# A Swin block and a dynamic convolution on one core: the first three rounds written out as one list, with cheaper weight folds and the early keys on ScalarE

## The chip, the cores and the metric

The kernel runs on one core of a Trainium2 chip. The metric is the device time of one execution in microseconds (us), from the first to the last instruction with what lies around them. The core has five engines with a queue each: TensorE (PE; its weight loads are PEld), VectorE (DVE), ScalarE (ACT), GpSimd (POOL) and SyncE (SP), which here only issues DMAs. All arithmetic is in float32.

## What is computed

The input is a batch of 16 images of 192 channels and 56 x 56 pixels. First comes a shifted-window attention block with its MLP, then a depthwise 3 x 3 convolution whose weights are computed from the image itself. Cut to what matters:

```python
# layer 0: shifted windows of 7 x 7, 6 heads of 32 channels
h = roll(layernorm(x over channels), -3, -3)          # norm 1
q, k, v = windows(h) @ qkv_w + qkv_b
a = softmax(q @ k.T * SCALE + rel_bias + window_mask)
x1 = x + roll(windows_back((a @ v) @ proj_w + proj_b), 3, 3)
y = gelu(layernorm(x1) @ fc1_w + fc1_b)               # norm 2
x2 = x1 + y @ fc2_w + fc2_b
# layer 1: masked depthwise 3 x 3 with weights per image and channel
t = relu(batchnorm(mean(x2 over pixels) @ w1.T))
taps = (t @ w2.T + b2) * mask                         # 4 of 9 taps stay
out = depthwise_conv(x2, taps) + bias
```

## The kernel before

**Tiling.** An image is cut into four steps; a step is two bands of seven rows (one row of windows each), so there are 64 steps. A tile has 128 partitions: one band on the first 64 (row half 0), the other on the last 64 (row half 1), and the 192 channels as three groups `g` of 64. Most products therefore use a half of TensorE's rows (`tile_position=(64 * ab, 0)`), and the two halves are issued in turn.

**Stages of a step s.** Norm 1: `statistics(0, s)` (L303) squares the rows on ScalarE and folds the three groups on GpSimd. Then the norm's product: either `full_deviations` (L392), which leaves mean and mean square on all 128 partitions (L398), after which ScalarE and VectorE make the reciprocal deviation in `rb` there; or `deviations(norms)` (L323), which does one or two norms in a few lanes (L333) and spreads them by a round trip through DRAM (one store, two loads on SP). `scaled1` (L435) multiplies the rows by it on GpSimd (L447, and L458 for the window that wraps round). `queries_keys` (L481) has three parts (products at L489): 0, queries of heads 0 to 3, copied by ScalarE (L502); 1, their keys, copied twice and masked by VectorE (L513); 2, heads 4 and 5, copied by ScalarE (L526, L536) and VectorE (L545). `scores` (L555) has three blocks j: product (L571), bias and maximum on VectorE (L597, L608), subtraction on GpSimd (L613), exponential on ScalarE (L620), sum and reciprocal on VectorE (L625, L626), share on GpSimd (L631). `turn_shares` (L635) turns them on VectorE (L642) and moves them by ten DMAs to `pt` (L648). `values` (L666) makes v in three groups (L686, copied by ScalarE, L702) and moves it by eight DMAs (L712); `turn_values` turns it (L721). `weighted` (L724) multiplies shares and values (L741), copied out by ScalarE (L768) or VectorE (L770). `biased_rows` (L779) adds a bias to the rows; `projection` (L786) multiplies (L812, L798) and VectorE adds to the rows (L840). Norm 2 is as norm 1, with `statistics(1, s)` and `scaled2` (L474). `first_layer` (L851, GELU at L863) and `second_layer` (L889) are the MLP; the convolution follows for each image.

**Weights.** The norms' gains and shifts are folded into the weights once. `centred_weights` (L1367) takes column means with products (L1378) and centres the weights on VectorE (L1407); `shift_steps` (L1338) multiplies weights by the norm's shift (products with one column, L1345), with the first row half only. `fold_qkv` and `fold_qkv_rest` do this for attention, `fold_v` (L1480) for the values' bias, `fold_fc1` for the first layer, and `fold_taps` prepares the convolution's weights.

**What sets the order.** The stages call `add(engine, planned duration, function, keys read, keys written)`. `Plan.order` then places all instructions: TensorE's stay in the order of the calls, the other engines take, at each moment of a planned timeline, a ready instruction by its latest due time. The order of the calls is therefore TensorE's order, and the planned durations and lags only steer the other queues. PSUM has four double banks, handed out in turn by `bank()`: a product waits until the one four banks earlier has been read. The calls come from a loop over rounds r from -2 (L1675): round r has scores and values of step r, the weighted sum and projection of step r - 1, the first layer of step r - 2 and the second layer of step r - 3. Rounds 0 to 2 deviate by many conditions (L1704 to L1780): the first steps use `full_deviations`, and step 0's third part of queries and keys stands between its second and third scores. `warm` (L193) issues products without use ahead of the first real ones.

Of the kernel before, what the change touches and what calls it, by code (L numbers as in the profile page):

```python
# [140 lines left out]
def tile_swin_then_dynamic_conv(  # L141
# [116 lines left out]
    mask2 = sb("mask2", 128, 2)  # L258
    km = sb("km", 128, 2)
    f1b = sb("f1b", 128, NFC)  # L260
    b1f = sb("b1f", 128, NFC)
# [219 lines left out]
    def queries_keys(s, parts):  # L481
        d = xs_of(s)[0]
        for i in parts:
# [26 lines left out]
            elif i == 1:  # L510
                for h in range(2):
                    def go(p=p, h=h):
                        nc.vector.tensor_scalar(  # L513
                            kbd[:, :, :, h, :],
                            p[:, :, 0:UT].rearrange("p a (w t) -> p a w t", t=N),
                            bq[:, 1:2],
                            mask2[:, h : h + 1],
                            ALU.add,
                            ALU.mult,
                        )  # L520
                    add("DVE", 1.0, go, [pk, "qb", "mask2"], [("kbd", h)])
# [32 lines left out]

    def scores(s, amid=None):  # L555

        last = s % NU == NU - 1
        for j in range(3):
            if j == 2 and amid is not None:
                amid()  # L560
            p, pk = bank()
# [70 lines left out]

            add("POOL", 1.9, share, [("tot", j)], [("e", j)])

    def turn_shares(s):  # L635
# [88 lines left out]
    def weighted(s):  # L724
# [25 lines left out]
        for j in range(3):  # L750
# [8 lines left out]
            for i in range(4):  # L759
# [5 lines left out]
                else:  # L765
                    dst = o2[lanes]
                if j != 1 or s < 2:
                    add("ACT", 0.5, lambda dst=dst, src=src: nc.scalar.copy(dst, src), [k], [("o", j, i)])  # L768
                else:
                    add("DVE", 0.56, lambda dst=dst, src=src: nc.vector.tensor_copy(dst, src), [k], [("o", j, i)])  # L770
# [566 lines left out]

    def shift_steps(n, chunks, p):  # L1338


        for c, lhs in enumerate(chunks):
            for g in range(G):
                to = 0
                for a in lhs(g):
                    nc.tensor.matmul(  # L1345
                        p[to : to + a.shape[1], 0, c : c + 1],
                        a,
                        vecs[0:64, 2 * n + 1, g : g + 1],
                        start=(g == 0),
                        stop=(g == G - 1),  # L1350
                        tile_position=(0, to),
                    )
                    to += a.shape[1]
            yield

    def shift_products(n, chunks, keys):
        p, pk = bank()
        add(
            "PE",
            0.68 * len(chunks),  # L1360
            lambda: list(shift_steps(n, chunks, p)),
            keys + [("vec", 2 * n + 1, 0)],
            [pk],
        )
        return p, pk

    def centred_weights(n, w, raw, keys, parts, chunks=()):  # L1367
# [3 lines left out]
        pm, mk = bank()  # L1371
        p, pk = bank() if chunks else (None, None)

        def means():
            shifts = shift_steps(n, chunks, p)
            for i, lo, hi, _ in parts:
                for g in range(G):
                    nc.tensor.matmul(  # L1378
# [6 lines left out]
                    )  # L1385
                    next(shifts, None)

        add(
            "PE",
            2.5 + 0.4 * len(chunks),  # L1390
            means,
            keys + [("gs", n)] + [("vec", 2 * n + 1, 0)] * bool(chunks),
            [mk, pk] if chunks else [mk],
        )

        for i, lo, hi, pieces_ in parts:
            for to, n_, view, done in pieces_:
                for g in range(G):
# [17 lines left out]
                    )  # L1416
        return p, pk

    qkv_keys = [("wqkvl", j) for j in range(2)]

    def fold_qkv():
# [24 lines left out]
        p, pk = shift_products(  # L1446
            0, [lambda g, i=i: [wraw[0:64, g, i * DIM : i * DIM + 128]] for i in range(2)], qkv_keys
        )

        def biases():  # L1450
            nc.vector.tensor_tensor(bq[:, 0:2], p[:, 0, 0:2], qkvb[:, 0:2], ALU.add)
            nc.vector.tensor_scalar(qbs[:, 0:1], bq[:, 0:1], SCALE, None, ALU.mult)

        add("DVE", 0.4, biases, [pk, "qkvb"], ["qb"])

    def fold_qkv_rest():
        p, pk = shift_products(
            0,
            [lambda g: [wraw[0:64, g, i * DIM + 128 : i * DIM + DIM] for i in range(2)]],
            qkv_keys,  # L1460
# [38 lines left out]
    def fold_fc1():  # L1499
        keys = [("wf1l", g, j) for g in range(G) for j in range(2)]  # L1500
        chunks = [lambda g, f=f: [wf1[0:64, g, f * 128 : (f + 1) * 128]] for f in range(NFC)]
        h = 2 * DIM
# [10 lines left out]
            0.2,  # L1513
            lambda: nc.vector.tensor_tensor(b1f, p[:, 0, 0:NFC], f1b, ALU.add),
            [pk, "f1b"],
# [150 lines left out]

    def last_heads():
        fold_qkv_rest()
        queries_keys(0, (2,))
        fold_v()  # L1670

    def has(s):
        return 0 <= s < S

    for r in range(-2, S + 3):  # L1675
        if r == -2:
            parameters_first()
            load(0, -100.0, 4.5)
            small_loads()
# [18 lines left out]
        if r == 0:  # L1698
            load(3)
            load_fc2()  # L1700
            load_taps()
        if has(r + 2) and r > -2:
            statistics(0, r + 2)
        early = r < 3  # L1704
        norms = [n for n, s in ((0, r + 2), (1, r - 1)) if has(s) and not early]
        if has(r) and r != 2:
            ahead = values(r)
            scores(r, {0: last_heads, 1: lambda: next(ahead)}.get(r))
            for _ in ahead:
                pass  # L1710
        if r == 2:
            scores(r)
            scaled1(3)
            queries_keys(3, (0, 1, 2))
            fold_fc1()
            full_deviations(1)
            scaled2(0)
            weighted(1)
        if r == 3:
            deviations([1])  # L1720
        if has(r - 2) and r > 2:
            scaled2(r - 2)
        if has(r + 1) and r > -2 and r != 2:
            if r == -1:
                warm(2, rb[:, 0], RB(0))
            scaled1(r + 1)
        if -2 < r < 2:
            if r == -1:
                warm(2, xs1[:, 0], [("xs1", 0)])
                queries_keys(0, (0, 1))  # L1730
            else:
                queries_keys(r + 1, (0, 1, 2))
            full_deviations()
        if has(r - 1) and r != 2:
            weighted(r - 1)
        if r == 1:
            ahead = values(2)
            for _ in range(G):
                next(ahead)
            fold_taps()  # L1740
        if has(r):
            turn_shares(r)
            turn_values()
        if r == 1:
            for _ in ahead:
                pass
        if r == S + 2:
# [15 lines left out]
        if has(r - 1):  # L1763
# [4 lines left out]
            statistics(1, r - 1)  # L1768
        if r == 2:
            full_deviations()  # L1770
        if weighing:
            halos(b)
        if not early and has(r + 1):
            queries_keys(r + 1, (0, 1, 2))
        if has(r - 2):
            table("gelu_and_others")
            first_layer(r - 2)
            table("natural_log_exp_and_others")
        if norms:
# [97 lines left out]
```

## Time and profile before

| | us |
|---|---|
| median of 3 runs (lowest, highest) | 2739.83 (2738.79, 2743.73) |
| the profiled execution | 2740.57 |
| its span, first to last instruction | 2738.5 |
| mean granted TensorE clock | 0.995 of full speed |
| VectorE, ScalarE, GpSimd busy | 1959.8, 1717.2, 1555.3 |
| first product of step 0's queries starts | 21.60 |
| first scores | 28.41 |
| first weighted sum | 67.35 |
| fold of the first layer's weights starts | 90.92 |
| first layer of step 0 starts | 114.38 |
| weighted sum of step 2 starts | 132.39 |

The rows with a start are from the trace, in us from the start of the span. A line of a view names a source line, the engine and what it writes and reads. A releaser ("<-") is what ended the idle time before an instruction. A matmul in float32 is recorded as two instructions, so 36 records of L489 are 18 products. Times come from one execution; the runs beside it lie within 5 us of each other.

### The profile page before, as it was taken

To read this page: it belongs to the slowest core of one execution; us is meant where nothing else is said; L and a number is where in the kernel's file an instruction comes from. 1 tells how busy PE (TensorE), PEld (TensorE's weight loads), DVE (VectorE), ACT (ScalarE), POOL (GpSimd) and SP (SyncE) were. 2 spreads that over 40 slices of the span, in tenths; PEclk is the share of its full clock that TensorE was granted. 3 is DMA by queue.
4 is the path that set the end of the run, shared out by engine and by line. 5 is a ranking of instruction groups with operands and counts; after the bars stand their busy time and mean duration, and the time that the engine had idled before them with its cause. 6 is when DMAs were issued, how large, how long until landed. Compare 5 with 4: busy or idle time off the path is not lost.

```text
span 2738.5 us, 78187 instructions
## 1 busy us (share of the span) xinstructions
PE 2707.5 (99%) x32911; PEld 1667.4 (61%) x32911; DVE 1959.8 (72%) x3457; ACT 1717.2 (63%) x2795; POOL 1555.3 (57%) x1433
## 2 busy tenths in 40 slices
PE   8999999999999999999999999999999999999998
PEld 5656656656666666566566566566566566666654
DVE  7656877767687676776767777676876767767674
ACT  4655666657666666666657666566666666676553
POOL 6656555555565565564565565565655655655532
PEclk9899999999999999999999999999999999999999
DMA  6522342434425334343344424344253343433231
GB/s 136 120 55 62 89 107 68 95 74 104 93 67 126 68 79 110 67 115 77 78 97 92 105 67 103 70 100 93 67 131 67 75 110 82 110 74 73 60 78 52
DMA packets 140603, 239.40 MB, mean 87 GB/s; under 512 B 34216, under 2 KB 98268, under 8 KB 140252
## 3 DMA queue, kind: packets, MB, share of 16 engines
q1 hardware_dynamic: 139100, 232.67, 37.9%
q8 instruction: 258, 4.23, 0.7%
q10 hardware_dynamic: 1152, 1.74, 0.3%
q14 instruction: 93, 0.76, 0.1%
HBM read 66.61 MB, written 38.98 MB: 39 GB/s over the span
## 4 chain that ended last, share of the span: by engine, by line
PE 96%; DVE 2%; DMA 1%; ACT 1%; SPq 0%; issue 0%; POOL 0%; ACTq 0%; DVEq 0%
PE ps L889 28%; PE ps L851 28%; PE ps L489 14%; PE ps L686 7%; PE ps L571 5%; PE ps L741 5%; PE ps L812 5%; PE ps L798 2%; PE ps L333 2%; DVE sq L985 0%; DMA x<-in_x_dram 0%; DVE x L840 0%; DVE hid L1165 0%; DVE trow L984 0%; ACT o L768 0%
## 5 line engine op out<-in xcount | busy, mean ns | idle before, releaser
L889 PE MATMUL ps<-hid,wf 128*64 128x392 f32 x4608 | 774.2, 494 | 0.4 <-issue 0.4
L851 PE MATMUL ps<-xs,wf 64*128 64x392 f32 x4608 | 769.5, 489 | 0.0
L851 PEld LDWEIGHTS ps<-xs,wf 64*128 64x128 f32 x4608 | 445.9, 187 | 312.9 <-POOL xs L474 1.2
L889 PEld LDWEIGHTS ps<-hid,wf 128*64 128x64 f32 x4608 | 327.8, 137 | 410.4 <-issue 379.3
L317 POOL TENSOR_TENSOR fold<-sq 128x392 f32<-128x392 f32 x127 | 129.6, 1020 | 702.3 <-PE ps L333 678.1
L631 POOL TENSOR_TENSOR e<-e,tot 128x784 f32<-128x784 f32 x192 | 324.0, 1698 | 203.8 <-DVE tot L626 197.7
L863 ACT ACTIVATE hid<-ps,b1f 128x784 f32<-128x784 f32 x384 | 341.9, 913 | 137.7 <-PE ps L851 135.3
L489 PE MATMUL ps<-xs,wqkv 64*128 64x392 f32 x2304 | 400.3, 496 | 3.2 <-DVE x L840 2.5
L1165 DVE SCALAR_TENSOR_TENSOR y<-x,wt,y 128x770 f32<-128x770 f32 x270 | 312.7, 1177 | 66.1 <-ACT y L1027 45.2
L489 PEld LDWEIGHTS ps<-xs,wqkv 64*128 64x128 f32 x2304 | 216.4, 187 | 164.8 <-issue 13.0
L613 POOL TENSOR_TENSOR e<-e,top 128x784 f32<-128x784 f32 x192 | 283.7, 1504 | 45.0 <-DVE top L608 44.9
L502 ACT ACTIVATE q<-ps,qbs 128x400 f32<-128x400 f32 (+1 forms) x128 | 68.3, 588 | 318.2 <-PE ps L489 315.3
L625 DVE TENSOR_REDUCE tot<-e 128x16 f32<-128x784 f32 x192 | 182.1, 949 | 107.7 <-ACT e L620 107.7
L768 ACT COPY o<-ps 32x392 f32<-32x392 f32 x520 | 247.6, 476 | 8.4 <-PE ps L741 2.1
L642 DVE STREAM_TRANSPOSE tt<-e 128x512 f32<-128x512 f32 x384 | 245.9, 684 | 2.2 <-POOL e L631 0.7
L779 ACT ACTIVATE x<-x,vecs 128x392 f32<-128x392 f32 x192 | 105.9, 613 | 207.6 <-POOL xs L458 207.6
L354 DVE TENSOR_TENSOR m<-ps,m 128x196 f32<-128x196 f32 (+1 forms) x63 | 22.8, 362 | 273.9 <-ACT m L347 273.8
L474 POOL TENSOR_TENSOR xs<-x,rb 128x392 f32<-128x392 f32 x192 | 193.8, 1039 | 28.6 <-DMA rb<-rsd 24.9
L686 PE MATMUL ps<-xs,wqkv 64*64 64x196 f32 x4608 | 205.2, 327 | 3.3 <-ACT q L526 1.4
L447 POOL TENSOR_TENSOR xs<-x,rb 128x343 f32<-128x343 f32 x191 | 185.9, 1002 | 32.0 <-DMA rb<-rsd 15.0
L317 POOL TENSOR_TENSOR fold<-x 128x392 f32<-128x392 f32 x128 | 132.8, 1037 | 100.2 <-DVE x L840 81.6
L597 DVE TENSOR_TENSOR e<-ps,bt 128x784 f32<-128x784 f32 x192 | 175.7, 968 | 12.3 <-ACT hid L863 6.2
(144 smaller groups left out, 3705.2 us busy)
## 6 DMA issues: line engine op xcount, KB each, us to landing
pt<-tt SPq DMA_DIRECT2D x256, 192.0 KB
vb<-kbd SPq DMA_DIRECT2D x488, 96.0 KB
x<-in_x_dram SPq DMA_DIRECT2D x112, 294.0 KB
out_dram<-y SPq DMA_DIRECT2D x135, 196.0 KB
pt<-tt SPq DMA_DIRECT2D x256, 96.0 KB
rb<-rsd SPq DMA_DIRECT2D x118, 196.0 KB
out_dram<-y SPq DMA_DIRECT2D x45, 154.0 KB
x<-in_x_dram SPq DMA_DIRECT2D x16, 168.0 KB
```

What stands on the lines that cost most here:

```text
L317: at.tensor_tensor(f, src[:, 0], src[:, 1], ALU.add)
L474: nc.gpsimd.tensor_tensor(xs2[:, g], xv[:, g], rb[:, 1], ALU.mult)
L489: nc.tensor.matmul(p[:, ab, 0:UT], lhs_qk(ab, g, i), d[P(ab), g, 0:UT], start=(g == 0), stop=(g == G - 1), tile_position=(64 * ab, 0),)
L613: nc.gpsimd.tensor_tensor(ev, ev, top[j].broadcast_to([128, 16, N]), ALU.subtract)
L631: nc.gpsimd.tensor_tensor(ev, ev, tot[j].broadcast_to([128, 16, N]), ALU.mult)
L642: nc.vector.transpose(tt[:, kb, 16 * j : 16 * j + 16], src)
L686: nc.tensor.matmul(p[P(wh), ab, 0 : 4 * N], wqkv[P(ab), g, 2 * DIM + 64 * m : 2 * DIM + 64 * m + 64], xs[P(ab), g, wh * 4 * N : (wh + 1) * ...
L768: add("ACT", 0.5, lambda dst=dst, src=src: nc.scalar.copy(dst, src), [k], [("o", j, i)])
L851: nc.tensor.matmul(p[:, ab, 0:UT], wf1[P(ab), g, f * 128 : (f + 1) * 128], xs2[P(ab), g], start=(g == 0), stop=(g == G - 1), tile_position ...
L863: nc.scalar.activation(hid[:, f], p[:, :, 0:UT], AF.Gelu, bias=b1f[:, f : f + 1])
L889: nc.tensor.matmul(p[P(ab), 0, 0:UT], wf2[:, f, g * 64 : (g + 1) * 64], hid[:, f, ab], start=(f == 0), stop=(f == NFC - 1), tile_position= ...
L1165: nc.vector.scalar_tensor_tensor(dst, s_, w[:, g, t : t + 1], dst, ALU.mult, ALU.add)
```

## The change

It has four parts. (1) Rounds 0 to 2 of the loop are replaced by `first_rounds`, one list of calls: scores and values of a step are now generators, taken block by block and mixed with other steps' products; the loop goes on with round 3. What rounds 0 to 2 did is done there, and also step 3's scores and values, which were round 3's. (2) In `shift_steps` and `centred_weights` products alternate between the two row halves, and shifts use both halves of the weights; in the first layer's fold the shifts follow the means and share their bank. (3) For steps 0 to 2 part 1's key copies are done by ScalarE, with a masked bias `kb` made once; the copies of step 1's weighted sum for j = 1 go to VectorE. (4) Step 4's first norm is no longer a `full_deviations`: it shares one `deviations([0, 1])` with step 1's second norm. Beside these, the second warm product reads fewer columns, and some planned durations change.

```diff
             elif i == 1:
                 for h in range(2):
+                    if s < 3:
+                        def go(p=p, h=h):
+                            nc.scalar.activation(
+                                kbd[:, :, :, h, :],
+                                p[:, :, 0:UT].rearrange("p a (w t) -> p a w t", t=N),
+                                AF.Identity,
+                                bias=kb[:, h : h + 1],
+                                scale=mask2[:, h : h + 1],
+                            )
+                        add("ACT", 0.95, go, [pk, "qb", "mask2"], [("kbd", h)])
+                        continue
...
-                if j != 1 or s < 2:
+                if j != 1 or s == 0:
                     add("ACT", 0.5, lambda dst=dst, src=src: nc.scalar.copy(dst, src), [k], [("o", j, i)])
...
-    def shift_steps(n, chunks, p):
-        for c, lhs in enumerate(chunks):
+    def shift_steps(n, chunks, p, first=0):
+        for c in range(0, len(chunks), 2):
             for g in range(G):
-                to = 0
-                for a in lhs(g):
-                    nc.tensor.matmul(
-                        p[to : to + a.shape[1], 0, c : c + 1],
-                        a,
-                        vecs[0:64, 2 * n + 1, g : g + 1],
-                        tile_position=(0, to),
+                for i, chunk in enumerate(chunks[c : c + 2]):
+                    to = 0
+                    for a in chunk(i, g):
+                        at = first + c // 2
+                        nc.tensor.matmul(
+                            p[to : to + a.shape[1], i, at : at + 1],
+                            a,
+                            vecs[P(i), 2 * n + 1, g : g + 1],
+                            tile_position=(64 * i, to),
...
         def means():
-            shifts = shift_steps(n, chunks, p)
-            for i, lo, hi, _ in parts:
-                for g in range(G):
+            for g in range(G):
+                for i, lo, hi, _ in parts:
                     nc.tensor.matmul(
                         pm[:, i, 0 : hi - lo],
...
-                    next(shifts, None)
+            shift_steps(n, chunks, pm, parts[0][2] - parts[0][1])
...
             nc.vector.tensor_scalar(qbs[:, 0:1], bq[:, 0:1], SCALE, None, ALU.mult)
+            nc.vector.tensor_tensor(kb, mask2, bq[:, 1:2].broadcast_to([128, 2]), ALU.mult)
...
+    def network_in(s):
+        table("gelu_and_others")
+        first_layer(s)
+        table("natural_log_exp_and_others")
+
+    def first_rounds():
+        v, qk = [[f(s) for s in range(4)] for f in (values, scores)]
+        scaled1(1)
+        next(qk[0])
+        fold_qkv_rest()
+        statistics(0, 2)
+        fold_v()
+        queries_keys(0, (2,))
+        next(v[0])
+        biased_rows(0)
+        next(qk[0])
+        next(v[0])
+        next(qk[0])
+        turn_shares(0)
+        next(v[0])
+        queries_keys(1, (0, 1))
+        full_deviations()
+        scaled1(2)
+        next(qk[1])
+        load(4)
+        next(v[0], None)
+        next(v[1])
+        next(v[1])
+        queries_keys(1, (2,))
+        biased_rows(1)
+        next(v[1])
+        next(qk[1])
+        queries_keys(2, (0, 1))
+        statistics(0, 3)
+        next(qk[1])
+        turn_values()
+        weighted(0)
+        turn_shares(1)
+        next(qk[2])
+        next(v[1], None)
+        full_deviations()
+        next(v[2])
+        next(qk[2])
+        next(v[2])
+        turn_values()
+        queries_keys(2, (2,))
+        for _ in projection(0):
+            pass
+        next(v[2])
+        next(v[2], None)
+        fold_fc1()
+        scaled1(3)
+        queries_keys(3, (0, 1))
+        fold_taps()
+        statistics(1, 0)
+        full_deviations(1)
+        next(qk[2])
+        weighted(1)
+        statistics(0, 4)
+        turn_shares(2)
+        load(5)
+        queries_keys(3, (2,))
+        scaled2(0)
+        for _ in projection(1):
+            pass
+        network_in(0)
+        next(qk[3])
+        turn_values()
+        next(qk[3])
+        next(v[3])
+        statistics(1, 1)
+        deviations([0, 1])
+        next(v[3])
+        next(v[3])
+        next(v[3], None)
+        next(qk[3])
...
-            load(0, -100.0, 4.5)
+            load(0, -100.0, 5.6)
...
+            first_rounds()
+        if 0 <= r < 3:
+            continue
...
-                warm(2, xs1[:, 0], [("xs1", 0)])
+            warm(2, xs1[:, 0, 0 : (NWIN - 1) * N], [("xs1", 0)])
```

The rest of the diff fits the loop, `scores` (a `yield` after each block), the callers of the folds and their planned durations to this.

## The prediction

> **What bounds the kernel now.** First the page's busy line and its forty slices: TensorE is busy nearly all the time, so a change can win only where it is idle or slow, or by giving it less to do.
>
> ```profile
> PE 2707.5 (99%) x32911; PEld 1667.4 (61%) x32911; DVE 1959.8 (72%) x3457; ACT 1717.2 (63%) x2795; POOL 1555.3 (57%) x1433
> ```
>
> Then the busy times by stretch, cut at the first product of step 0's queries (21.60) and at the first layer of step 0 (114.38); after the length come the busy times of PE, PEld, DVE, ACT and POOL, the granted clock, the DMA share and GB/s.
>
> ```profile
> 0.00:21.60 21.60, 17.34 (x68) 11.81 (x68) 10.11 (x32) 3.90 (x5) 13.09 (x23) 0.92 0.61 127
> 21.60:114.38 92.78, 80.03 (x1058) 54.75 (x1057) 73.40 (x124) 57.81 (x114) 57.65 (x55) 0.89 0.65 140
> 114.38:132.39 18.01, 18.01 (x252) 11.95 (x255) 10.99 (x22) 13.82 (x19) 11.85 (x11) 1.00 0.35 69
> 132.39:173.70 41.31, 41.31 (x517) 25.46 (x520) 23.79 (x48) 25.25 (x43) 22.76 (x23) 1.00 0.26 55
> ```
>
> Only the second stretch is loose: 12.75 us of idle TensorE and a clock of 0.89. A mean of 0.89 is half speed for 0.11/0.5 of 92.78 = 20.4 us, so some 10 us more are lost. A full round (last line) has no hole, and the change leaves its list as it is. Next, who TensorE waits for in the first 450 us (total, times, longest):
>
> ```profile
> PE ps L571 <- ACT q L526: 2.7, 2, 2.3
> ...
> PE ps L812 <- ACT o L768: 1.7, 2, 1.4
> ...
> PE ps L571 <- DVE kbd L513: 1.1, 1, 1.1
> PE ps L686 <- DVE e L597: 1.1, 1, 1.1
> ```
>
> No single wait: scores wait for their queries and keys, projections for output copies, and values for PSUM banks not yet read. Last, the chain, which in round 4 is TensorE alone and so prices each product at full clock (start, length):
>
> ```profile
> 149.76 6.12 PE ps L489 x36
> 155.88 11.85 PE ps L851 x72
> 167.74 0.80 PE ps L333 x16
> 168.54 2.19 PE ps L571 x96
> 170.73 2.98 PE ps L686 x72
> 173.72 2.06 PE ps L741 x96
> ...
> 187.78 1.99 PE ps L812 x24
> 189.77 1.16 PE ps L798 x24
> ```
>
> **The work in the loose stretch.** Four steps' queries and keys 4 x 6.12 = 24.5; three scores 6.6; three values 8.9; two weighted sums 4.1; two projections 6.3; five whole-array norms at 1.51 (the last runs from 112.79 to 114.30) 7.6; two small bias products 1.6; taps 0.3; fc1's fold 7.9 (six steps at the 1.31 us that the timeline shows before the clock falls). Sum 67.8 us of 92.78: 25 us are waits and slow clock.
>
> **Part by part.**
>
> *fc1's fold.* Its means and shifts lie from 90.92 to 99.27. The means now alternate between row halves: at the rate of L489, whose halves alternate (36 in 6.12), twelve take 2.0 us. The 36 shift products lie between two rows. Now, on one half with 128 columns, twelve take 1.32 us (L1345 in the qkv fold), 110 ns each; L1480, both halves and 64 columns, does 36 in 1.30, 36 ns each. The Trainium skill ("TensorE: Matmul & The Clock Gate", LDWEIGHTS) prices a load by its columns, columns/1.2 ns: 107 for 128, and 53 for L1480's 64. The first agrees, but L1480 beats its 53, so loads of different halves overlap. By the rule 36 x 107 = 3.9 us; by L1480 doubled for the columns 2.6. I take 2.6 (bounds 1.3 and 3.9): the fold costs 4.6 instead of 7.9.
>
> *Norms.* Step 4's first norm loses its 1.51 us product and joins step 1's second, whose half product (L333) costs the same 0.80 with one norm or two. ScalarE and VectorE lose its four instructions (1.65 and 0.57). It rides in the store and the two loads on SP that step 1's second norm made already; its reader, step 4's product, is 20 us of products away. Its folding on GpSimd, 4 x 1.02, stays. Taken -1.5 us, bounds -1.5 and +1.
>
> *Early keys on ScalarE.* Six L513 at 1.09 us leave VectorE (-6.5). On ScalarE the nearest row is L863, 0.91 us for the same 784 columns from PSUM; the ceiling is two L536 halves, 1.36. Taken 0.95, so +5.7 there. Behind these in ScalarE's queue stand value copies and exponentials. The keys of one step now end 1.9 us after their product. The four copies of step 1 that go back to VectorE cost it 4 x 0.56 = 2.3 and spare ScalarE 1.9. The new `kb` lies between 0.15 (L1465) and 0.67 (L1466); I take 0.4, on the way to the first keys only.
>
> *The start.* TensorE's second warm product waits at 20.09 for the last window (POOL L458, end 20.03) and runs until 21.60, when the real product starts. It now reads only columns that L447 wrote earlier, so it fits into the wait: -1.5 us, bounds -1.5 and 0 (weights being centred until 21.35 may hold the product). The qkv fold's shifts shrink too, worth nothing: POOL sets the start.
>
> *The list.* I walk it from 20.1 with the prices above.
> - The first norm waits for POOL's fold until 25.2: 1 us idle. First scores at 26.7 (now 28.4).
> - The third part's keys and queries alternate between ScalarE and VectorE: product end at 32.4, last scores of step 0 at 36.78, 4.4 us. That wait now holds values and a score (2.7 us): 1.7 idle.
> - The scores of step 1 follow their keys' product by one norm, 1.5 us against 1.9: 0.5 idle.
> - weighted(0) comes 19 us after step 0's last scores, against 30.6 now (36.78 to 67.35). Its chain by rows: bias and maximum 1.93, subtraction 1.50, power 0.86, sum and reciprocal 1.20, share 1.50, turn 1.37, ten SP issues 6.5, landing 2: 16.9 if nothing queues. Something will: 3 idle (bounds 0 and 11.5), and every later product stands behind it in TensorE's queue.
> - Behind it the norm, values and scores take the banks that weighted(0)'s copies free, twelve at 0.48 on ScalarE: 3 idle.
> - Step 0's second norm (adds 3.0, square 1.2, folds 4.1) and projection(1) (output copies): 1 and 1.7.
>
> That is 12 us. Work: 67.8 - 3.3 - 1.5 = 63.0. Step 3's scores and values stay behind the first layer, so the 18.01 us after it stay 18.
>
> The load of step 4 moves up on SP, two issues of 0.65, and step 5's likewise; SP has gaps (54.9 to 58.0 waiting for turns), so I count nothing; with no gap it is 1.3 us ahead of one set of shares.
>
> *The clock.* The same page of the skill ("Why this matters for your kernels") asks for no TensorE gap over about 3 us. By that rule this kernel should not have slowed after 21.6, and the new order would be free of it. The trace disagrees: gaps of 2.35 us (before 36.0) and a group of 0.75 us (72 to 77) were enough, and in fc1's fold the clock fell with TensorE busy throughout:
>
> ```profile
> 94.00:96.00 2.00, 2.00 (x14) 1.86 (x14) 1.54 (x2) 1.58 (x3) 0.32 (x1) 0.59 1.08 178
> 96.00:98.00 2.00, 2.00 (x16) 2.00 (x15) 1.00 (x2) 0.00 (x0) 1.92 (x3) 0.50 0.52 96
> ```
>
> Now there are four slow spells, three of 3.4 us and one of 10.4 (94.4 to 104.8). The trace decides: with gaps of 2 to 3 us left and a shorter fold I count two spells of 3.5 us, in which half the time is lost, 3.5 us; by the rule nothing.
>
> Sum: 63.0 + 12 + 3.5 = 78.5 from 20.1, so the first layer starts at 98.6 instead of 114.38, 15.8 us sooner. A cross-check by VectorE: its 73.4 us become 73.4 - 6.5 + 2.3 + 0.4 = 69.6; in 78.5 us that is 89% full, against 79% now. That is tight, so I take 15. From the profiled execution, 2740.57 (span 2738.5 and 2.1 around it), that is 2725.6; from the median of the runs, 2739.83, 2724.8. Forecast 2725.
>
> **Rivals.**
> - *VectorE stays as full as it is.* Nothing shows that order alone fills it: 69.6/0.79 = 88 us, first layer at 108 to 109.7, gain 5 to 6: 2734. For it: its idle time now is short waits on three engines. Against: much of them is waiting for TensorE. Chance 0.17.
> - *The waits vanish.* The walk with half its idle time and a full clock: 63 + 6 = 69, gain 25; VectorE would need to be full (69.6), so I take 22: 2718. Chance 0.16.
> - *ScalarE becomes the bound, slower.* It gets 57.8 + 5.7 - 1.9 = 61.6 us. If its fill stays at today's 62% (57.8/92.8), they take 99 us, first layer at 119 (from 20.1) to 120.5 (from 21.6), 5 to 6 us later: 2745. It decides below a fill of 65% (61.6 in the 94.3 us from 20.1 to 114.38). For it: keys stand in its queue behind waiting instructions. Against: it idles now because products come late (8.6 us for norms, 6.3 for the third part). Chance 0.06.
> - *The order doesn't matter* (each hole closed opens another: the chain of shares at today's 30.6 us in both early steps, and late value copies): gain 0 to 5: 2737. Chance 0.06.
>
> The likeliest, gain 9 to 19, has 0.55.
>
> **How the numbers follow.** What can be told from no change is 0.2%, 5.5 us. Faster: 0.55 + 0.16 + most of VectorE's case (0.15) = 0.86. Same 0.08, slower 0.06. The range runs from the second rival's better half (gain 25, 2715) to a gain of 5 (2735); what it leaves out is both last rivals and a little of the others.
>
> **What would show it.** Right: the first layer at 95 to 103; weighted(0) before 62; the first queries' product at about 20.1; fc1's fold in 4 to 5 us; VectorE near 0.9 full up to the first layer; rounds of 41.3 us after it, without holes. Wrong: idle TensorE before weighted(0) over 6 us (the chain of shares), fc1's fold over 6 us, four slow spells or more, or the early gain handed back in rounds 3 and 4 by waits for norms that come through DRAM.

## The result, and the profile after

| | before | changed |
|---|---|---|
| median of the runs beside each other (lowest, highest) | 2739.94 us (2738.79, 2743.73) | 2723.78 us (2721.45, 2728.37) |
| the profiled execution (its span) | 2740.57 (2738.5) | 2723.80 (2721.8) |
| first product of step 0's queries | 21.6 | 20.1 |
| first weighted sum | 67.4 | 60.3 |
| fold of the first layer's weights starts | 90.9 | 76.0 |
| first layer of step 0 starts | 114.4 | 94.7 |
| weighted sum of step 2 starts | 132.4 | 112.9 |

Six runs each: 16.2 us less, a ratio of 0.9941 [0.9928, 0.9954]. The forecast was 2725 in a range of 2715 to 2735. By the page's busy line TensorE is 13.3 us less busy and the others almost as before; a product at half clock counts as busy for twice as long, so this is not all less work.

```profile
PE 2694.2 (99%) x32915; PEld 1655.0 (61%) x32915; DVE 1957.5 (72%) x3455; ACT 1719.3 (63%) x2794; POOL 1552.5 (57%) x1433
```

The busy times by stretch, cut at the same products as before (first queries 20.1, first layer 94.66), with the columns as before: length, PE, PEld, DVE, ACT, POOL, clock, DMA share, GB/s.

```profile
0.00:20.10 20.10, 15.46 (x68) 10.64 (x68) 9.25 (x32) 2.93 (x4) 12.26 (x22) 1.00 0.53 109
20.10:94.66 74.56, 67.83 (x1053) 44.99 (x1053) 63.97 (x113) 59.58 (x112) 56.99 (x54) 0.98 0.72 155
94.66:112.85 18.19, 18.19 (x265) 12.15 (x269) 13.97 (x31) 14.58 (x22) 10.53 (x10) 1.00 0.89 182
112.85:154.16 41.31, 41.31 (x524) 25.46 (x521) 25.01 (x48) 25.03 (x43) 25.50 (x25) 1.00 0.28 59
```

The second stretch went from 92.78 to 74.56 us: idle TensorE from 12.75 to 6.73 us, the clock from 0.89 to 0.98. By the record of the clock there is one slow spell left in it, 3.4 us from 30.9, where there were four (20.4 us). So TensorE is 6.0 us less idle and 12.2 us less busy in this stretch; half of the 17 us of slow clock that went makes 8.5 of the 12.2, which leaves an estimated 3.7 us of less work. VectorE is now 63.97/74.56 = 86% full there, against 79%. The full round of the last line is 41.31 us as before. The waits of TensorE in the first 450 us (total, times, longest; without the L200 rows, which are warm products ahead of 20.1):

```profile
PE ps L581 <- ACT kbd L515: 1.8, 2, 1.3
PE ps L581 <- ACT q L538: 1.6, 1, 1.6
PE ps L399 <- POOL fold L320: 1.5, 3, 0.7
PE ps L581 <- ACT o L779: 0.7, 1, 0.7
PE ps L752 <- DVE tot L636: 0.4, 1, 0.4
...
```

The longest is the last scores of step 0 for their queries (1.6). Step 0's weighted sum (L752) waits 0.4. The chain (start, length) names the products by line, fold and first layer among them:

```profile
60.26 2.45 PE ps L752 x93
...
76.02 2.20 PE ps L1389 x12
78.22 1.91 PE ps L1359 x35
80.12 4.06 PE ps L490 x24
...
85.86 0.84 PE ps L581 x32
86.70 2.48 PE ps L752 x96
...
94.66 12.05 PE ps L862 x72
...
112.85 2.09 PE ps L752 x96
```

The means (L1389) and shifts (L1359) of the first layer's fold take 4.1 us together, against 8.35 before; by the record of the clock neither they nor the products behind them run slow.

From the first layer on the changed kernel needs 3.0 us more than before to the end of its span (2721.8 - 94.66 = 2627.1 against 2738.5 - 114.38 = 2624.1). So the lead is 19.7 us at the first layer and 16.7 at the end of the span.

### The profile page after: what moved, and what is told of

It is laid out like the page before. It is cut to its first block, busy times and chain, and to the rows that moved or that the text cites. A ratio compares the mean times of both kernels' runs of the same rounds, so it can differ in the third digit from the quotient of the medians.

```text
span 2721.8 us, 78193 instructions
## 1 busy us (share of the span) xinstructions
PE 2694.2 (99%) x32915; PEld 1655.0 (61%) x32915; DVE 1957.5 (72%) x3455; ACT 1719.3 (63%) x2794; POOL 1552.5 (57%) x1433
## 4 chain that ended last, share of the span: by engine, by line
PE 96%; DVE 2%; DMA 1%; ACT 1%; issue 0%; SPq 0%; ACTq 0%; DVEq 0%
PE ps L900 28%; PE ps L862 28%; PE ps L490 13%; PE ps L697 7%; PE ps L581 5%; PE ps L752 5%; PE ps L823 5%; PE ps L809 2%; PE ps L334 2%; DVE trow L995 1%; DVE sq L996 0%; DVE x L851 0%; DMA x<-in_x_dram 0%; DVE hid L1176 0%; DMA hid<-in_L_conv_norm_b_dram 0%
## 5 line engine op out<-in xcount | busy, mean ns | idle before, releaser
L1176 DVE SCALAR_TENSOR_TENSOR y<-x,wt,y 128x770 f32<-128x770 f32 x270 | 316.9, 1193 | 66.1 <-ACT y L1038 45.2
L790 ACT ACTIVATE x<-x,vecs 128x392 f32<-128x392 f32 x192 | 105.7, 612 | 217.5 <-POOL xs L459 215.7
```

Source lines behind the costliest of these rows:

```text
L1176: nc.vector.scalar_tensor_tensor(dst, s_, w[:, g, t : t + 1], dst, ALU.mult, ALU.add)
```

## The experiments

The theory: the gain is the early stretch alone; the order of the list, the folds and ScalarE's keys each remove a different wait or slow spell on one chain of products. Rivals: one part does nearly everything; or the parts are fungible, each worth its share of engine time wherever it is put. Times are medians; before beside them lay at 2739.8 to 2739.9.

### Parts undone or done alone

**The list alone** (old folds, keys and norm, and the smaller edits undone):

```diff
-                    if s < 3:
+                    if s < 0:
...
-                if j != 1 or s == 0:
+                if j != 1 or s < 2:
...
         for _ in projection(1):
             pass
+        full_deviations()
         network_in(0)
...
-        deviations([0, 1])
+        deviations([1])
```

> The new list of calls with the other parts undone: folds on one row half as before, early keys and step 1's output copies as before, step 4's first norm on the whole array (behind projection(1)), warm-up over all columns. Theory (the list itself closes most of the holes): the first layer starts 94.7 + 1.5 (start) + 3.8 (fold's work) + 1.5 (norm) + some 3 (slow clock in the fold) + 1.5 (keys) = near 106, 8 us before the old 114.4, so about 2731 us. Rival (the gain is mostly less work and a better clock in the fold, the list brings little): first layer after 110, 2735 us or more.

2735.11 us in 21 runs, 0.9983 [0.9977, 0.9990]: only 4.8 us, as the rival had it. TensorE waits 5.7 us at step 0's weighted sum (the same wait comes back below with the keys alone), and the first layer starts at 110.8. And the clock fell in the fold as before. Busy times in two stretches of it:

```profile
86.00:90.00 4.00, 4.00 (x23) 3.45 (x22) 1.14 (x2) 1.56 (x3) 4.00 (x5) 0.50 1.05 186
90.00:94.00 4.00, 4.00 (x21) 3.80 (x21) 2.52 (x5) 0.00 (x0) 2.70 (x2) 0.50 0.56 129
```

TensorE is busy all of it at half clock; the last idle time over 0.25 us before it ends at 66.0.

**The list undone** (before's order, with the new folds, keys on ScalarE, copies and warm product):

```diff
-            first_rounds()
-        if 0 <= r < 3:
-            continue
+        # the loop's rounds 0 to 2 as in the kernel before
```

> The old rounds and their order, with the other parts: folds on both row halves, early keys on ScalarE, step 1's copies on VectorE, the narrower warm-up; step 4's first norm stays on the whole array. Theory (waits take back what the parts save while the order is old): gain of 5 to 8 us on before, 2732 to 2735. Rival (fold and clock carry the change): gain of 12 or more, 2728 or less. In both, the slow spell of 10.4 us inside the fold should shrink to one window or none.

2738.16 us, 0.9993 [0.9985, 1.0001], which can't be told from no change; 5 to 8 us had been expected. Its fold is as cheap as planned and the next waiting product takes it back. The products in order (start, length, waits in brackets):

```profile
91.96 2.10 PE L1390 MATMUL ps<-wf,gs 64*128 64x384 f32 x12
93.89 2.07 PE L1360 MATMUL ps<-vecs,wf 64*128 64x1 f32 x36
95.89 1.58 PE L399 MATMUL ps<-fold,hid 128*128 128x392 f32 x4
100.44 3.36 PE L753 MATMUL ps<-pt,v 49*64 49x100 f32 x96 [2.96 <-DVE b1f L1527]
```

The fold takes 4.0 us, 4 less than before; then step 1's weighted sum waits 2.96 us and runs in a slow spell. Up to the first layer (111.6) TensorE is idle for 16.9 us in all. So in the old order the cheaper parts buy waiting time. The two runs gain 4.8 + 1.7 = 6.5 us, the whole 16.2. Neither has step 4's norm shared, which is worth 0 to 1.6 us (below). The parts are not a sum: each one's worth depends on the others.

**The old folds** in the changed kernel:

```diff
-            for g in range(G):
-                for i, lo, hi, _ in parts:
+            shifts = shift_steps(n, chunks, p)
+            for i, lo, hi, _ in parts:
+                for g in range(G):
...
+                    next(shifts, None)
```

> The changed kernel with only the folds back on one row half (shifts between the means, as before). Theory (narrow products on one half slow the clock by themselves, though TensorE shows as busy): the fold takes 8 us or more again and a slow spell of one to three windows of 3.4 us lies in and behind it, though no gap precedes it: 6 to 9 us slower than the changed kernel, 2730 to 2733. Rival (the old slow spell came from gaps ahead of it): clock stays at 1.00 there, only 3.8 us slower, 2727.6.

2731.92 us, 0.9967 [0.9954, 0.9979]: 8.1 us more than the changed kernel. In four stretches of 4 us around the fold, which starts at 80.6:

```profile
76.00:80.00 4.00, 4.00 (x66) 3.13 (x68) 3.63 (x7) 2.21 (x5) 2.75 (x2) 1.00 1.01 202
80.00:84.00 4.00, 4.00 (x36) 2.88 (x28) 3.96 (x15) 3.29 (x7) 4.00 (x7) 1.00 0.83 176
84.00:88.00 4.00, 4.00 (x34) 4.00 (x34) 3.71 (x7) 1.40 (x3) 4.00 (x5) 0.70 0.81 135
88.00:92.00 4.00, 4.00 (x14) 3.59 (x13) 2.85 (x7) 0.34 (x1) 2.54 (x2) 0.50 0.63 151
```

PE is full in every row and no gap over 0.25 us lies after 74.1; yet from 85.6 the clock is at half for 6.8 us, and the queries behind the fold, 4.1 us in the changed kernel, take 6.6. So the old fold costs twice: 2.3 to 2.7 us itself (6.4 to 6.8 against 4.1), and 2.5 at the queries behind it. That is about half of the 10.2 us by which its first layer is later (104.8). The fold itself starts 4.5 us later: ahead of it this execution has longer waits (3.5 instead of 1.6 at step 0's last scores, 3.1 instead of 0.4 at its weighted sum) and a slow spell of 6.8 us from 61.7. Whether the fold's form brings these stays open.

**Early keys back on VectorE:**

```diff
-                    if s < 3:
+                    if s < 0:
```

> The changed kernel with only the early keys back on VectorE (6 x 1.09 us). Theory (VectorE is the tightest engine in the early rounds, 86% full up to the first layer): first layer 2 to 5 us later, 2726 to 2729. Rival (VectorE has room, and on ScalarE the keys stand behind other work: 1.9 us behind a bias that waited): first scores earlier than 28.6, first layer within 1 us of 94.7, 2723 to 2725.

2734.58 us in 12 runs, 0.9980 [0.9971, 0.9988]: 10.8 us more, where 2 to 5 had been expected. The profiled execution was the slowest of these runs, so a second one was profiled:

> The run with all early keys on VectorE once more, for a second trace. If the wait at the first weighted sum belongs to the order, it is 5 to 6 us again, behind a last turn of step 0 that ends near 57.7; if it was chance, it is under 2.

2733.77 us. Both executions show the same long wait (5.64 and 5.68 us) at step 0's weighted sum. The waits of TensorE from 20 to 125 us, of the second execution:

```profile
PE ps L752 <- DVE tot L636: 5.7, 1, 5.7
PE ps L581 <- DVE kbd L525: 3.4, 2, 2.6
PE ps L752 <- DMA pt<-tt: 2.5, 1, 2.5
```

The releaser named (a reciprocal done long before) is not the cause, as VectorE and SP show. VectorE's timeline in this kernel:

```profile
45.61 2.09 DVE L525 TENSOR_SCALAR kbd<-ps,bq,mask 128x784 f32<-128x784 f32 x2 [0.31 <-PE ps L490]
...
50.38 0.96 DVE L635 TENSOR_REDUCE tot<-e 128x16 f32<-128x784 f32 x1
...
55.90 1.29 DVE L653 STREAM_TRANSPOSE tt<-e 128x512 f32<-128x512 f32 x2
```

and in the changed kernel, where no key copy stands ahead of the sum of the last block:

```profile
45.56 0.95 DVE L635 TENSOR_REDUCE tot<-e 128x16 f32<-128x784 f32 x1
46.55 0.25 DVE L636 RECIPROCAL tot<-tot 128x16 f32<-128x16 f32 x1
46.72 1.24 DVE L653 STREAM_TRANSPOSE tt<-e 128x512 f32<-128x512 f32 x2
...
49.21 2.47 DVE L653 STREAM_TRANSPOSE tt<-e 128x512 f32<-128x512 f32 x4
```

SP's sends of turned shares of steps 0 and 1, with the keys on VectorE:

```profile
56.63 7.02 SPq L659 DMA_DIRECT2D pt<-tt  x10
...
85.28 7.62 SPq L659 DMA_DIRECT2D pt<-tt  x10
```

and in the changed kernel:

```profile
51.12 6.62 SPq L659 DMA_DIRECT2D pt<-tt  x10
...
75.43 7.53 SPq L659 DMA_DIRECT2D pt<-tt  x10
```

Step 1's two key copies (2.1 us) enter VectorE's queue between the blocks of step 0's shares. Two turns and two other instructions then also go ahead of the last block's sum, which comes at 50.4 instead of 45.6. Its turns end at 57.2 instead of 51.7, the sends start at 56.6 instead of 51.1, and the weighted sum at 66.0 instead of 60.3. The gap then costs a second time: the clock is at half from 65.0 for 6.8 us, 3.4 us of work lost. Of these 9 us some are won back from shorter waits, so the fold starts 6.8 us later (82.8). Then step 1's weighted sum repeats it: its sends start at 85.3 instead of 75.4, it waits 2.5 us at 96.0 (the third row of the waits), and the clock is at half from 95.7 for another 6.8 us. So the first layer is 12.3 us later (106.9).

**Step 4's first norm as it was**, a full product by itself:

```diff
+        full_deviations()
         network_in(0)
...
-        deviations([0, 1])
+        deviations([1])
```

> The changed kernel with step 4's first norm again on the whole array (behind projection(1)) and step 1's second norm alone. Theory (only its product, 1.51 us, and the four instructions behind it come back, in a stretch without holes): first layer 1.5 to 2 us later, 2725 to 2726. Rival (the fold that it needs earlier, step 4's, is late and opens a hole ahead of the first layer): 3 us or more, 2727 or more.

2725.38 us, 0.9946 [0.9932, 0.9960]. Beside the changed kernel's two medians (2723.8, and 2725.3 below) the difference of 0.1 to 1.6 us can't be told from nothing.

### The start

```diff
-            warm(2, xs1[:, 0, 0 : (NWIN - 1) * N], [("xs1", 0)])
+            warm(2, xs1[:, 0], XS1(0))
```

> The changed kernel with the second warm-up again over all columns, behind the last window of the scaled rows. Theory (the start was held by this product): first queries at 21.6 instead of 20.1. What of these 1.5 us reaches the first layer: the first norm waits for GpSimd until 25 anyway, so 0 to 1.5 us; 2724 to 2725.5. Rival (the weights' centring holds the start): first queries still at 20.1.

2728.02 us, 0.9952 [0.9939, 0.9964]; five runs from 2720.65 to 2729.72, the profiled one the lowest. The first queries start at 22.0 there, 1.9 us late, but the first layer at 94.4, as in the changed kernel: the first scores wait for their keys in both, and start at 28.5 and 28.6. Its median can't be told from the changed kernel's. At the start itself the traces do show the gain: all three kernels with the wide product have a slow spell of 3.4 us at 9 to 11 us and start at 21.6 to 22.2, while the two traces with the narrow product and such a spell there (the list undone, the norm as it was) start at 20.5 and 20.4. But it does not reach the first layer in this execution.

### Place or load: keys by steps

Is it the place (step 1's keys stand between step 0's shares) or VectorE's load? ScalarE takes the keys of step 1 alone, then those of steps 1 and 2:

```diff
-                    if s < 3:
+                    if s == 1:
```

> The changed kernel with only step 1's keys on ScalarE, those of steps 0 and 2 on VectorE. Theory (it is the place: step 1's keys stand between the shares of step 0 in VectorE's queue and push its last turn, and so the first weighted sum, back by 6 us): the first weighted sum within 2 us of 60.2, wait there under 2, 2723 to 2727. Rival (it is VectorE's load as a whole): two thirds of the loss of the run with all keys on VectorE, first layer near 102, 2730 to 2732.

2732.77 us in 19 runs, 0.9977 [0.9970, 0.9985]; its profiled execution was the slowest of them (2740.67).

```diff
-                    if s < 3:
+                    if s in (1, 2):
```

> The changed kernel with the keys of steps 1 and 2 on ScalarE and only step 0's on VectorE. Theory (each step's keys on VectorE push back the next weighted sum: step 1's the first, step 2's the second; step 0's push only the first scores): first and second weighted sums within 2 us of 60.2 and 86.7, waits there under 1, 2724 to 2727. Rival (it is VectorE's whole load): one third of the loss of the run with all keys on VectorE, 2727 to 2729, with a wait at a weighted sum.

2729.59 us, 0.9967 [0.9955, 0.9979]. The ladder, by steps whose keys ScalarE copies: none 2734.6, step 1 2732.8, steps 1 and 2 2729.6, all 2723.8. The weighted sum of step 0 follows the place: with step 1's keys gone it starts at 60.8 and 61.2 and waits 0.8 and 1.3 us. The time does not: both runs miss what would follow from the place (2723 to 2727) and lie a little above what would follow from the load (2730 to 2732, and 2727 to 2729). The first rung, 1.8 us, is within the spread of the runs; from steps 1 and 2 to all the step is clear, though step 0's keys stand among no step's shares. TensorE's waits from 20 to 125 us with the keys of steps 1 and 2 on ScalarE:

```profile
PE ps L581 <- DVE kbd L525: 2.6, 1, 2.6
PE ps L752 <- DMA pt<-tt: 2.6, 1, 2.6
```

The first wait is the first scores' for step 0's own keys, which VectorE reaches late (1.3 us with ScalarE). It costs little: the first layer starts at 95.1, as in the changed kernel. The loss lies behind it. The second wait is step 2's weighted sum at 116.0, which waits for its shares' landing: their sends start at 106.6 us instead of 103.0, and a slow spell of 6.8 us follows. VectorE's timeline in this kernel says what step 0's keys pushed back:

```profile
65.55 1.34 DVE L1589 TENSOR_TENSOR bt<-hid 128x294 f32<-128x294 f32 x1
...
78.63 0.54 DVE L1589 TENSOR_TENSOR bt<-hid 128x98 f32<-128x98 f32 x1
```

These are bias tables, which in both traces of the changed kernel are done by 63.2 us. With step 1's keys alone on ScalarE they last until 90.0, with none until 90.6. So a key copy displaces work that has no hurry, and this work later stands among another step's shares. That this carries the loss to step 2 is read from single traces and was not tried by an edit.

### Two fills of the remaining waits

**The row bias behind the early keys.** In the changed kernel the first scores wait 1.34 us because ScalarE takes the row bias (L790) ahead of the keys. ScalarE's timeline there:

```profile
25.60 1.14 ACT L790 ACTIVATE x<-x,vecs 128x392 f32<-128x392 f32 x2 [1.73 <-DVE f1b L1279]
26.64 1.89 ACT L515 ACTIVATE kbd<-ps,kb,mask 128x784 f32<-128x784 f32 x2
```

and VectorE's:

```profile
24.47 0.96 DVE L1589 TENSOR_TENSOR bt<-hid 128x294 f32<-128x294 f32 x1 [3.72 <-DMA hid<-relrows]
25.35 0.15 DVE L1278 COPY vecs<-ps 128x15 f32<-128x15 f32 x1
```

The bias waits for `vecs`, whose copy (0.15 us) stands in VectorE's queue behind a bias table that waits 3.72 us for its DMA; the keys, whose product was done at 24.3, stand behind the bias. The edit makes step 0's row bias wait for the later query bias, so that the planner puts the keys first:

```diff
-                ["vecs"],
+                ["vecs"] + ["qb2"] * (s == 0),
```

> The changed kernel with only the row bias of step 0 kept behind the third part's biases; value products in the order of the change. Theory (in the run with both, the moved value product waited for the PSUM bank that the third part's copies free, and so pushed the last scores and the first weighted sum): without the move the wait at the first weighted sum is under 1 us again, first scores 0.8 to 1.5 us sooner after the first queries than in the changed kernel, first layer 73 to 74 us after the first queries instead of 74.5; 2722 to 2724. Rival: the wait at the first weighted sum stays at 2 to 4.

2726.02 us, 0.9952 [0.9939, 0.9964], not faster. In its profiled execution, the slowest of its five (2730.7), the first scores do start at 26.5, 6.6 us behind the first queries instead of 8.5, but the next part of queries and keys waits 2.75 us for a bank that a reciprocal deviation on VectorE frees. VectorE's timeline in this kernel:

```profile
24.80 4.70 DVE L1589 TENSOR_TENSOR bt<-hid 128x98 f32<-128x98 f32 x5
...
30.84 0.56 DVE L414 TENSOR_TENSOR rb<-ps,rb 128x392 f32<-128x392 f32 x1
```

L414 stands behind the bias tables, 6 us of them. Step 0's weighted sum then starts at 64.8 with a wait of 4.3, a slow spell of 6.8 us lies at 30.8, and the first layer starts at 100.1. The expectation was wrong: while the first scores waited, VectorE worked at tables that now hold TensorE up one product later.

**A value product ahead of step 0's last scores**, beside the edit of the row bias:

```diff
-        next(qk[0])
         next(v[0])
         next(qk[0])
+        next(v[0])
+        next(qk[0])
         turn_shares(0)
-        next(v[0])
```

> The changed kernel with two holes filled: the row bias of step 0 waits for the third part's biases, so that it no longer stands ahead of the first keys on ScalarE, and step 0's last value product goes ahead of its last scores. Theory: first scores at 27 instead of 28.6, the wait ahead of the last scores 0.6 instead of 1.6; first layer at 92 to 93, 2721 to 2722. Rival (the chain of shares, 0.45 us from being the wait at the first weighted sum, takes it back there): the wait at the first weighted sum grows to 1.5 or more and the first layer stays at 94 to 95, 2724.

2727.37 us, 0.9962 [0.9950, 0.9975]. The moved product waits instead, for the PSUM bank that the third part's query copies free:

```profile
37.27 1.23 PE L697 MATMUL ps<-xs,wqkv 64*64 64x196 f32 x24 [1.92 <-ACT q L538]
```

The wait changed its line (1.6 at the scores, 1.9 here), and step 0's weighted sum came at 61.7, waiting 3.6. No version of these runs beats the changed kernel.

### The changed kernel once more

The same code, unaltered:

> The changed kernel once more, unaltered, for the spread of its runs and for a second trace. Expected: 2724 within 2; the first layer within 2 us of 94.6; if slow spells hang on where the clock's 3.4 us windows happen to lie, their places differ from the first trace, and so do the short waits in the later rounds.

2725.30 us in five runs from 2719.71 to 2727.41, 0.9946 [0.9934, 0.9959]. In its profiled execution the first queries start at 22.1, step 0's weighted sum at 61.7 (waiting 1.0), step 1's at 89.7 (waiting 1.6), the first layer at 97.8; a slow spell lies at 38.7 instead of 30.9, and another from 8.0 to 14.8. The first layer moved 3.1 us later between two executions of one kernel with times 1.5 us apart. So a row of one trace is good to some 3 us here. The eleven runs of this kernel span 2719.7 to 2728.4, and the interval of a ratio from five runs is some 3.5 us to each side, so differences of less than that between two such medians show nothing.

## Why the prediction was right, point by point

*The first layer.* Predicted 98.6 by the walk (15.8 us sooner), found 94.7 and, once more, 97.8: at the early end of the 95 to 103 named as right, and 0.3 ahead of it. The time came out at the forecast because the lead, 3.9 us larger than the sum, was partly handed back behind it (3.0). That the total fits to 1.2 us is therefore in part luck: idle time and slow clock were taken too high, work too low, and nothing was taken for the hand-back. The terms of the stretch, the first trace against the sum:

| term | predicted | first trace |
|---|---|---|
| work at full clock | 63.0 | 66.1 |
| idle TensorE | 12 | 6.7 |
| slow clock | 3.5 | 1.7 |
| from first queries to first layer | 78.5 | 74.6 |

*Work, 3.1 us short.* I priced each product at its length in a round, where blocks of one kind stand in a row. In the mixed list they stand alone: a block of scores takes 0.84 to 0.91 us instead of 2.19/3 = 0.73, some 1.4 us for the stretch; the first two weighted sums take 2.5 instead of 2.06 (0.8; before's own first one took 1.83 and 0.92 in two pieces, a row I passed over for round 4's). By the chain the two pieces of a step's queries and keys take 4.06 to 4.2 and 2.2 instead of 6.12 together (an estimated 0.9 for four steps), and a group of values alone 1.0 to 1.3 instead of 2.98/3 = 0.99 (an estimated 0.7). The fold returned 0.5.

*The fold of fc1* was right: 4.6 predicted, 4.1 found. Its 36 shifts take 1.91 us in the chain, 53 ns each. By the Trainium skill's price for a load ("TensorE: Matmul & The Clock Gate", LDWEIGHTS; columns/1.2, 107 ns) one after the other would be an estimated 3.9; the trace decides for loads that overlap when row halves alternate, as L1480 had hinted (2.6 taken).

*Idle TensorE* was the term most mis-sized: 6.7 against 12, close to the 6 of the rival that the waits vanish. I took 3 us at step 0's weighted sum, 3 behind it for banks and 2.7 at step 0's second norm and projection(1); found were 0.45, 1.2 and 0. Of the listed holes, three came true to a tenth or two: first norm 1.1 (1), step 0's last scores 1.6 (1.7), step 1's scores 0.5 (0.5). One was missed: 1.3 at the first scores, which I had without a wait, because I did not walk ScalarE's queue past the row bias and the DMA behind it. In the second trace idle TensorE was 8.3.

*Early keys on ScalarE* were priced rightly per instruction (0.95 taken, 0.96 found in pairs) and wrongly as a step: I entered them as 6.5 us off VectorE and 5.7 on ScalarE, and in the walk only where scores wait for keys. Undone, they cost 10.8 us. Where VectorE's queue takes them, or what they push back, decides when shares are turned, and so when the weighted sum may start; behind that wait (5.7) the clock falls (3.4). The bound of "0 and 11.5" at the weighted sum held it, the link to the keys did not appear.

*The clock.* Two spells counted, one seen in the stretch (in the other trace, one too). The rule of no gap over about 3 us (the Trainium skill, same page, "Why this matters for your kernels") is not enough here. It agrees at step 0's weighted sum, in the twelve traces with the new list: the six with a wait of 3.05 to 5.68 us there have a slow spell that begins within 1.1 us of the product, the six with 0.45 to 1.32 us none. But with the old folds the clock fell after 11 us with no gap over 0.25 us, and in the new kernel a wait of 1.34 us is the longest between the first queries and the spell at 30.9. In all three traces with the old folds (before, the list alone, the old folds) a spell begins in the fold. In all eleven with the new folds, it runs at full clock and takes 4.0 to 4.1 us (in one of them, step 1's keys alone on ScalarE, a spell begins 1.5 us behind it, after a wait of 0.8).

*Start:* 20.1 as predicted in the first trace. In the other traces with the narrow product it is 19.6 to 22.1; in the three late ones (21.8 to 22.1) the warm products before 15 us run at half speed. At equal clock the narrow product is worth 1.1 to 1.8 us at the start (above), but a gain in the time can't be shown.

*Step 4's norm:* taken -1.5, measured 0.1 to 1.6 by medians that don't resolve it.

*Rivals.* "VectorE stays as full as it is" said 2734 for a list that can't fill VectorE. With the keys on VectorE just that came. The busy times from 20 us to the first layer, of the second execution:

```profile
20.00:106.94 86.94, 72.81 (x1052) 50.31 (x1052) 69.06 (x121) 54.57 (x106) 58.14 (x54) 0.90 0.75 155
```

VectorE is 69.06/86.94 = 79% full, as before, and the time is 2733.8. So the rival was right about the list without ScalarE's keys, though by luck in its numbers: it took 69.6 us of VectorE with the keys moved, and the 69.06 are with the keys on it. That sum, also behind the cross-check of 89%, was too high: with the keys moved VectorE has 64.0 us in the stretch (66.1 in the second trace) and is 86% full. Part of the rest now stands behind the first layer (13.97 us in the next stretch, 10.99 before). "The waits vanish" (2718) had the idle time nearly right and failed by the work and the hand-back. "ScalarE becomes the bound" failed: ScalarE is 80% full (59.58/74.56) and its longest holds of TensorE are 1.3 and 1.6 us. "The order doesn't matter" is close to what the list alone gives (4.8).

*The gain handed back.* It was named among the things that would make the prediction wrong, by waits for norms in rounds 3 and 4. Not so: the first stretch after the first layer is 18.19 us (18 predicted) and a full round is unchanged. About half, 1.6 us, goes between the first layers of steps 0 and 12, 1.5 of it as one pause before the last product of a weighted sum at 531.5, for which the profile shows no wait; the rest is scattered over fifty rounds. In the trace with the norm alone it is 0.2 us, and in the second of the changed kernel 1.5. It was not tried by a run of its own; whether the change causes it, or one execution's chance, stays open.

## What to carry to other kernels

In a stretch that three engines nearly fill, walk every queue and not only TensorE's: a copy of 2 us that enters VectorE ahead of a long chain of later steps (sum, turn, send, land) costs what it delays at the end of that chain, and here a second time by the clock. Parts of a change that each remove one hole on the same path don't add: 4.8 and 1.7 us in two halves, 16.2 together, because a hole closed alone lets the next late buffer be waited for. Price a short product by rows where it stands as it will stand, alone among others, not by its share of a long run.

## What the runs showed of the hardware

- The clock can fall with TensorE busy: one-column products on one row half, 128 columns of weights each, ended at half clock in three kernels (from 94.4, 85.6 and 85.6 us); the same products on alternating halves stayed at 1.00 in eleven traces. What the chip measures for it isn't settled by these runs.
- Loads into different row halves overlap: 53 ns per one-column product with 128 columns of weights on alternating halves (36 in 1.91 us) against 110 on one half (L1345 before, 12 in 1.32 us).
- The slow spells of the first 200 us last 3.4, 6.8 or 10.2 us and start, in each trace, on a grid of 3.41 us (before: 9.03, 36.34, 77.30, 94.37 and 108.02, which are 8, 12, 5 and 4 steps apart). Their places move between executions of one kernel (30.9; 8.0 and 38.7).
- A key copy of 784 columns from PSUM takes ScalarE 1.00 us alone and 0.96 in a pair, VectorE 1.09 and 1.04.
